# A field-pair interaction kernel: loading five blocks of x by GpSimd's queue, 120 rows in one transfer

## The chip, the cores and the metric

The kernel runs on one core of a Trainium2 chip. The metric is the device time of one execution in microseconds (us). Three executions of the kernel before took 1344.6, 1345.8 and 1345.83 us; the median is 1345.8. The profile is of one execution, with a span of 1343.8 us from the program's first instruction to its last.

The core has a matrix engine (TensorE, PE, with its weight loads PEld), a vector engine (VectorE, DVE), a scalar engine (ScalarE, ACT), GpSimd (POOL) and SyncE (SP). Sixteen DMA engines move data between the main memory and the core's own memory. They are fed by queues: SyncE and ScalarE each have one whose transfers are expanded by hardware, GpSimd has one that software expands. A transfer is split over up to sixteen DMA engines, each does its share as a row of packets, and the transfer has landed when the last of them has reported to its semaphore.

## The reference

```python
B, F, D = (4096, 32, 64)              # inputs; W has F*(F-1)/2 = 496 matrices of D x D
idx_i, idx_j = np.triu_indices(F, k=1)
vi = inputs[:, idx_i, :]
vj = inputs[:, idx_j, :]
vidots = jnp.einsum('bpd,pde->bpe', vi, W)
return vidots * vj
```

For each of 4096 rows and each of the 496 pairs (i, j) of fields with i < j, field i's vector of 64 numbers goes through the pair's own matrix, and the result is multiplied element by element with field j's vector. The output, 4096 x 496 x 64 floats, is 520 MB; x is 33.6 MB and W 8.1 MB.

## The kernel before

The rows are cut into 16 blocks of 256. A block lies in the core's memory as `xs`, 128 partitions with two rows of x each (`NB` = 2), so a partition holds 2 x 32 x 64 floats, 16 KB; what one partition gets of a block is called a row from here on, and a block has 128 of them. There are two such buffers. A half of a block (one of the two rows of x in each partition) is a pass `t`; 32 passes are made. Of W, `wT` holds the whole, turned once at the start.

In a pass the kernel goes through the pairs in 46 steps. For a step, TensorE multiplies turned fields (`xT`) with a run of the matrices into PSUM (line 244); then VectorE multiplies that with field j from `xs` and writes the output buffer `ot` (line 261). For some steps (`aside`) ScalarE copies PSUM out (line 258) and GpSimd multiplies (line 259). A pass has five groups of pairs, and each group fills one `ot` buffer of up to 105 pairs, which SyncE's queue stores (line 266): 3,360 KB for the two largest groups. There are three `ot` buffers, so a group can be computed only when the store from three groups earlier has landed.

The blocks of x are loaded one block ahead: `loads` says at which step. Blocks 0 and 1 come at the start by SyncE's queue. Of the rest, ScalarE's queue brings most in one transfer of 128 rows of 16 KB (`load_x`, line 76). Blocks 4, 7, 10 and 13 come otherwise (`load_fifteen`, lines 95 to 105): rows 0 to 119 (`SWR` = 120) by GpSimd's queue in two transfers, each with half the fields of every row (line 103), and the last eight rows as two small transfers of five and three rows by ScalarE's queue (line 99). 

`turn_engines` (lines 86 to 93) issues a tiny copy by GpSimd's queue, of 5, 17 or 11 rows with two single floats each, into a scratch tile that nobody reads. Its purpose lies in how that queue deals shares to the DMA engines: a copy's number of shares moves on the place at which the next copy's shares begin. It is called with 5 at the start, with 1 (17 rows) after each half of a block in `load_fifteen`, and with 11 at the end. `keep_in_program_order` makes GpSimd issue these copies in the order of the source.

A block of x that is loaded is needed two passes later, when its first fields are turned (line 143); a load is issued in the seventh step of a pass (block 2 in pass 3, block b from 3 on in pass 2b - 2).

Of the kernel before, what the change touches and what calls it, by code (L numbers as in the profile page):

```python
# [12 lines left out]
def kernel(  # L13
# [16 lines left out]
    nc = tc.nc  # L30

    B, F, D = x.shape
    P = 128
# [30 lines left out]
    xs = {}  # L64

    def rows_of(dram: bass.AP, blk: int) -> bass.AP:
        return dram[blk * NB * P : (blk + 1) * NB * P]

    def new_x(blk: int):

        xs[blk] = xpool.tile([P, 1 + NB * F, D], F32, tag="xs", name=f"xs_{blk}")
        nc.gpsimd.memset(xs[blk][:, 0, :], 0.0)  # L72

    def load_x(blk: int, eng, k0: int = 0, k1: int = NB):
        src = rows_of(x, blk).rearrange("(p k) f d -> p (k f) d", k=NB)
        eng.dma_start(out=xs[blk][:, 1 + k0 * F : 1 + k1 * F, :], in_=src[:, k0 * F : k1 * F, :])
# [4 lines left out]
    SWR = 120  # L81
# [4 lines left out]
    def turn_engines(k: int):  # L86
        n = k if k > 1 else 17
        c = used[0] % 8
        used[0] += 1
        src = x[: NB * n].rearrange("(p k) f d -> p k f d", k=NB)  # L90
        tc.keep_in_program_order(
            nc.gpsimd.dma_start(out=scratch[:n, :, c : c + 1], in_=src[:, :, 0, 0:1])  # L92
        )

    def load_fifteen(blk: int):
        rows = rows_of(x, blk).rearrange("(p k) f d -> p k f d", k=NB)
        dst = xs[blk][:, 1:, :].rearrange("p (k f) d -> p k f d", k=NB)
        for a, b in ((SWR, SWR + 5), (SWR + 5, P)):
            nc.scalar.dma_start(out=xs[blk][a:b, 1:, :], in_=rows[a:b].rearrange("p k f d -> p (k f) d"))
        for h in range(2):  # L100
            cut = slice(h * F // 2, (h + 1) * F // 2)
            tc.keep_in_program_order(
                nc.gpsimd.dma_start(out=dst[:SWR, :, cut, :], in_=rows[:SWR, :, cut, :])  # L103
            )
            turn_engines(1)


    wflat = w.rearrange("p d e -> p (d e)")
# [4 lines left out]
    def load_w(c: int, eng=nc.sync):  # L113

        a, b = wrows[c]
        pool, tag = ((opool, "ot"), (opool, "ot"), (const, "w3"), (const, "w3"))[c]
        raw[c] = pool.tile([P, D * D], F32, tag=tag, name=f"raw_{c}")
        eng.dma_start(out=raw[c][: b - a, :], in_=wflat[a:b])

    def order_w(c: int, k: int, copy):  # L120
        r = wrows[c][1] - wrows[c][0]
        rp = tpool.tile([P, EU, 2, D], F32, tag="tmp", name=f"rp_{c}_{k}")
        src = raw[c][:r, :].rearrange("p (d h e) -> p e h d", h=2, d=D)
        copy(rp[:r], src[:, k * EU : (k + 1) * EU])  # L124
        return rp

    def turn_w(c: int, k: int, rp, copy):
        r = wrows[c][1] - wrows[c][0]
        if c not in wT:
            wT[c] = const.tile([P, r, E2], F32, tag=f"w{c}", name=f"wT_{c}")  # L130
        pt = psum.tile([P, EU, P], F32, tag="ps", name=f"ptw_{c}_{k}")
        for n in range(EU):
            nc.tensor.transpose(  # L133
                pt[:, n, :r], rp[:r, n].rearrange("p h d -> p (h d)"), ident[:r, :r]
            )
        copy(wT[c][:, :, k * EU : (k + 1) * EU], pt[:, :, :r].rearrange("p e r -> p r e"))  # L136

    def turn_x(blk: int, k: int, q: int, copy):

        pt = psum.tile([P, RUN, P], F32, tag="ps", name=f"ptx_{blk}_{k}_{q}")  # L140
        for n in range(RUN):
            s = k * F + q * RUN + n
            nc.tensor.transpose(  # L143
                pt[:, n, :], xs[blk][:, s : s + 2, :].rearrange("p f d -> p (f d)"), ident
            )
        xT = xtpool.tile([P, RUN, P], F32, tag="xT", name=f"xT_{blk}_{k}_{q}")
        copy(xT, pt)  # L147
        return xT
# [41 lines left out]
    loads = {place[blk * NB, LATE]: blk + 1 for blk in range(2, NBLK - 1)}  # L190
# [12 lines left out]
    v, p, a = nc.vector.tensor_copy, nc.gpsimd.tensor_copy, nc.scalar.copy  # L203
# [9 lines left out]
    for s, (t, st) in enumerate(sched):  # L213
        blk, kt = divmod(t, NB)
        g, i, c0, m = steps[st]
        if s in loads:
            new_x(loads[s])
            if loads[s] % 3 == 1:
                load_fifteen(loads[s])
            else:  # L220
                load_x(loads[s], nc.scalar)
        for what, *args in due.get(s, ()):
            if what == "x":
                xT[tuple(args)] = turn_x(*args, a)
            elif what == "turn":
                turn_w(*args, rps.pop(tuple(args)), a)
            else:
                c, k = args
                rps[c, k] = order_w(c, k, (v, v, p, v)[c] if k % 2 == 0 else (v, v, p, a)[c])
                if (c, k) == (2, NU - 1):  # L230
                    load_w(3, nc.scalar)

        base, end = groups[g]
        pa = p0[i] + c0
        if pa == base:
            ots[t] = opool.tile([P, cap, D], F32, tag="ot", name=f"ot_{t}_{g}")
        ot = ots[t]
        ps = psum.tile([P, 2, CH, E2], F32, tag="ps", name=f"ps_{s}")
        for c, (lo, hi) in enumerate(wrows):
            lo, hi = max(pa, lo), min(pa + m, hi)  # L240
            if lo < hi:
                for h in range(2):
                    n = i + 1 - h
                    nc.tensor.matmul(  # L244
                        ps[:, h, lo - pa : hi - pa, :],
                        xT[blk, kt, n // RUN][h * D : (h + 1) * D, n % RUN, :],
                        wT[c][h * D : (h + 1) * D, lo - wrows[c][0] : hi - wrows[c][0], :],
                        start=True,
                        stop=True,
                    )  # L250
        o = pa - base
        j = 1 + kt * F + i + 1 + c0
        dst = ot[:, o : o + m, :].rearrange("p m (h e) -> p m h e", h=2)
        src = ps[:, :, :m, :].rearrange("p h m e -> p m h e")
        xj = xs[blk][:, j : j + m, :].rearrange("p m (h e) -> p m h e", h=2)
        if i in aside and c0 == 0 and s not in no_aside:
            tmp = tpool.tile([P, CH, 2, E2], F32, tag="tmp", name=f"tmp_{s}")
            nc.scalar.copy(tmp, src)  # L258
            nc.gpsimd.tensor_mul(dst, tmp, xj)  # L259
        else:  # L260
            nc.vector.tensor_mul(dst, src, xj)  # L261

        ends = (p0[2], end) if s < NS and (t, g) == (0, 0) else (end,)
        if pa + m in ends:
            n0 = p0[2] if len(ends) > 1 and pa + m == end else base
            nc.sync.dma_start(
                out=rows_of(out, blk).rearrange("(p k) n d -> p k n d", k=NB)[:, kt, n0 : pa + m, :],
                in_=ot[:, n0 - base : pa + m - base, :],
            )
# [28 lines left out]
```

## Time and profile before

| what | us or share |
|---|---|
| median time | 1345.8 us |
| span of the profile | 1343.8 us |
| mean rate of the DMA engines | 419 GB/s |
| bytes written to main memory / read | 520.09 MB / 41.68 MB |
| VectorE busy | 956.0 us (71%) |
| GpSimd busy | 544.7 us (41%) |
| GpSimd's transfers of half-rows (line 103) | 8, 960 KB each, median 31.5 us from issue to landing |
| ScalarE's whole loads (line 76) | 10, 2048 KB each, 17.3 us |
| stores of the largest groups (line 266) | 64, 3360 KB each, 16.3 us |

The page gives each engine's busy time; the span in 40 slices, a digit for each, with the DMA engines' busy share in tenths; the queues with packets, megabytes and the share of sixteen engines' time; the chain of work that ended last, followed back from the end; and a list of who waited for whom, with the total in us, the number of times and the longest wait. [...]

### The profile page before, as it was taken

How to read it: one execution, taken by the hardware profiler on the slowest of the kernel's cores; microseconds unless marked ns; L12 is line 12 of the kernel's file. 1: busy time of each engine (PE TensorE's matmuls, PEld its weight loads, DVE VectorE, ACT ScalarE, POOL GpSimd, SP SyncE). 2: the span in 40 equal slices, each digit the busy share in tenths (PEclk: the TensorE clock that was granted, in tenths of full speed). 3: DMA queues.
4: the chain of work that ended last, by engine and by line, in shares of the span. 5: the costliest groups of instructions: out<-in, count | busy, mean ns of one | idle time of the engine just before them, and what ended most of it. 6: DMA issues, size and time to landing. Idle time of an engine off the chain costs nothing.

```text
span 1343.8 us, 17902 instructions
## 1 busy us (share of the span) xinstructions
PE 1163.9 (87%) x7424; PEld 680.1 (51%) x7424; DVE 956.0 (71%) x1262; ACT 374.1 (28%) x367; POOL 544.7 (41%) x264
## 2 busy tenths in 40 slices
PE   6989889888898888888889888888988889989894
PEld 4555545545455454455445554444554545545552
DVE  5778767766677677776758777576876767767774
ACT  3432222223232232222232222232222323223321
POOL 1813424444243445333444434442444424344431
PEclk9989999999999899998989999899899989989997
DMA  9999999999999999999999999999999999999997
GB/s 394 371 427 410 427 422 433 429 421 430 422 430 426 431 427 407 427 424 429 432 420 424 404 424 431 425 430 416 419 421 411 428 425 427 423 423 431 423 415 320
DMA packets 28258, 562.95 MB, mean 419 GB/s; under 512 B 3456, under 2 KB 3456, under 8 KB 5504
## 3 DMA queue, kind: packets, MB, share of 16 engines
q1 hardware_dynamic: 24048, 530.59, 93.0%
q10 hardware_dynamic: 1632, 23.33, 4.2%
q0 software_dynamic: 2496, 7.88, 1.5%
q8 instruction: 58, 0.95, 0.3%
q14 instruction: 24, 0.20, 0.0%
HBM read 41.68 MB, written 520.09 MB: 418 GB/s over the span
## 4 chain that ended last, share of the span: by engine, by line
DMA 50%; PE 23%; DVE 16%; POOL 6%; issue 3%; ACT 1%; DVEq 0%; SPq 0%; POOLq 0%; ACTq 0%
DMA out_dram<-ot 50%; PE ps L244 18%; DVE ot L261 16%; POOL ot L259 5%; PE ptx L143 4%; PE ptw L133 1%; DMA raw<-in_L_rec_W_dram 1%; POOL scratch L92 1%; ACT tmp L258 1%; POOL xs L103 0%; DVE rp L124 0%; POOL rp L124 0%; DVEq L261 0%; ACT wT L136 0%; POOL xs L72 0%
## 5 line engine op out<-in xcount | busy, mean ns | idle before, releaser
L261 DVE TENSOR_TENSOR ot<-ps,xs 128x1024 f32<-128x1024 f32 (+15 forms) x1252 | 944.8, 810 | 356.8 <-DMA out_dram<-ot 193.8
L244 PE MATMUL ps<-wT,xT 64*128 64x512 f32 (+13 forms) x6272 | 1017.8, 467 | 122.4 <-DVE ot L261 110.7
L244 PEld LDWEIGHTS ps<-wT,xT 64*128 64x128 f32 x6272 | 552.7, 193 | 553.1 <-DVE ot L261 289.0
L259 POOL TENSOR_TENSOR ot<-tmp,xs 128x1024 f32<-128x1024 f32 x220 | 519.0, 2360 | 622.1 <-ACT tmp L258 438.7
L258 ACT COPY tmp<-ps 128x1024 f32<-128x1024 f32 x220 | 222.7, 1012 | 468.3 <-PE ps L244 401.2
L147 ACT COPY xT<-ptx 128x1024 f32<-128x1024 f32 x128 | 129.5, 1012 | 451.1 <-PE ptx L143 451.1
L143 PE MATMUL ptx<-ident,xs 128*128 128x128 f32 x1024 | 142.0, 283 | 35.9 <-DVE ot L261 27.5
L143 PEld LDWEIGHTS ptx<-ident,xs 128*128 128x128 f32 x1024 | 111.8, 143 | 82.5 <-issue 41.9
L72 POOL MEMSET xs<- 128x64 f32 x16 | 2.4, 151 | 148.5 <-DVE ot L261 148.5
L133 PE MATMUL ptw<-ident,rp 128*128 128x128 f32 (+1 forms) x128 | 18.6, 298 | 3.9 <-DVE rp L124 3.9
L133 PEld LDWEIGHTS ptw<-ident,rp 128*128 128x128 f32 (+1 forms) x128 | 15.6, 156 | 10.3 <-DVE rp L124 5.0
L136 ACT COPY wT<-ptw 128x1024 f32<-128x1024 f32 (+1 forms) x15 | 14.8, 984 | 20.9 <-PE ptw L133 20.9
L124 DVE COPY rp<-raw 128x1024 f32<-128x1024 f32 (+1 forms) x9 | 10.7, 1221 | 10.8 <-DMA raw<-in_L_rec_W_dram 10.8
L92 POOL DMA_DIRECT2D scratch<-in_r_inputs_dram x10 | 9.1, 908 | 0.2 <-issue 0.2
L124 POOL COPY rp<-raw 128x1024 f32<-128x1024 f32 x4 | 7.9, 1979 | 0.1
L124 ACT COPY rp<-raw 112x1024 f32<-112x1024 f32 (+1 forms) x3 | 5.9, 1958 | 5.0 <-POOL ot L259 3.2
L103 POOL DMA_DIRECT2D xs<-in_r_inputs_dram x8 | 6.0, 753 | 1.4 <-issue 1.4
L136 DVE COPY wT<-ptw 128x1024 f32<-128x1024 f32 x1 | 1.2, 1224 | 2.9 <-PE ptw L133 2.9
L147 ACT ACT_TABLE_LOAD x1 | 1.3, 1283 | 0.7 <-PEq L285 0.7
masks.py:197 POOL MEMSET ident<- 128x128 f32 x1 | 0.2, 204 | 0.3 <-POOLq L285 0.3
masks.py:199 POOL TENSOR_SCALAR_AFFINE_SELECT ident<-ident 128x128 f32<-128x128 f32 x1 | 0.3, 288 | 0.0
L285 POOL MEMSET const-float32-0.0<- 128x1 f32 x1 | 0.1, 93 | 0.3 <-issue 0.3
(3 smaller groups left out, 0.3 us busy)
## 6 DMA issues: line engine op xcount, KB each, us to landing
out_dram<-ot SPq DMA_DIRECT2D x64, 3360.0 KB, 16.3
out_dram<-ot SPq DMA_DIRECT2D x32, 3168.0 KB, 16.4
out_dram<-ot SPq DMA_DIRECT2D x32, 3104.0 KB, 17.0
out_dram<-ot SPq DMA_DIRECT2D x31, 2880.0 KB, 17.1
xs<-in_r_inputs_dram ACTq DMA_DIRECT2D x10, 2048.0 KB, 17.3
xs<-in_r_inputs_dram POOLq DMA_DIRECT2D x8, 960.0 KB, 31.5
raw<-in_L_rec_W_dram SPq DMA_DIRECT2D x3, 2048.0 KB, 17.1
xs<-in_r_inputs_dram SPq DMA_DIRECT2D x2, 1024.0 KB, 5.2
```

Of the source, the lines that this page charges most:

```text
L72: nc.gpsimd.memset(xs[blk][:, 0, :], 0.0)
L92: nc.gpsimd.dma_start(out=scratch[:n, :, c : c + 1], in_=src[:, :, 0, 0:1])
L103: nc.gpsimd.dma_start(out=dst[:SWR, :, cut, :], in_=rows[:SWR, :, cut, :])
L124: copy(rp[:r], src[:, k * EU : (k + 1) * EU])
L133: nc.tensor.transpose(pt[:, n, :r], rp[:r, n].rearrange("p h d -> p (h d)"), ident[:r, :r])
L136: copy(wT[c][:, :, k * EU : (k + 1) * EU], pt[:, :, :r].rearrange("p e r -> p r e"))
L143: nc.tensor.transpose(pt[:, n, :], xs[blk][:, s : s + 2, :].rearrange("p f d -> p (f d)"), ident)
L147: copy(xT, pt)
L244: nc.tensor.matmul(ps[:, h, lo - pa : hi - pa, :], xT[blk, kt, n // RUN][h * D : (h + 1) * D, n % RUN, :], wT[c][h * D : (h + 1) * D, lo - ...
L258: nc.scalar.copy(tmp, src)
L259: nc.gpsimd.tensor_mul(dst, tmp, xj)
L261: nc.vector.tensor_mul(dst, src, xj)
```

## The change

`load_fifteen` takes the blocks whose number is divisible by three (3, 6, 9, 12 and 15) in place of 4, 7, 10 and 13. In it, rows 0 to 119 go in one transfer with all fields. After one `turn_engines(1)`, the last eight rows follow on GpSimd's queue too, as two transfers with half the fields each, so ScalarE's queue has no part in these blocks. It is meant to spread the load of x over the sixteen DMA engines in a different way: with fewer transfers and with no whole rows on a few engines.

```diff
     def load_fifteen(blk: int):
         rows = rows_of(x, blk).rearrange("(p k) f d -> p k f d", k=NB)
         dst = xs[blk][:, 1:, :].rearrange("p (k f) d -> p k f d", k=NB)
-        for a, b in ((SWR, SWR + 5), (SWR + 5, P)):
-            nc.scalar.dma_start(out=xs[blk][a:b, 1:, :], in_=rows[a:b].rearrange("p k f d -> p (k f) d"))
+
+        def part(ps: slice, fs: slice):
+            tc.keep_in_program_order(nc.gpsimd.dma_start(out=dst[ps, :, fs, :], in_=rows[ps, :, fs, :]))
+
+        part(slice(0, SWR), slice(0, F))
+        turn_engines(1)
         for h in range(2):
-            cut = slice(h * F // 2, (h + 1) * F // 2)
-            tc.keep_in_program_order(
-                nc.gpsimd.dma_start(out=dst[:SWR, :, cut, :], in_=rows[:SWR, :, cut, :])
-            )
-            turn_engines(1)
+            part(slice(SWR, P), slice(h * F // 2, (h + 1) * F // 2))
...
-            if loads[s] % 3 == 1:
+            if loads[s] % 3 == 0:
                 load_fifteen(loads[s])
             else:
                 load_x(loads[s], nc.scalar)
```

## The prediction

> **What bounds the kernel now.** First the page's parts 1 to 3, which say which resource is full.
>
> ```profile
> PE 1163.9 (87%) x7424; PEld 680.1 (51%) x7424; DVE 956.0 (71%) x1262; ACT 374.1 (28%) x367; POOL 544.7 (41%) x264
> ...
> DMA  9999999999999999999999999999999999999997
> ...
> q1 hardware_dynamic: 24048, 530.59, 93.0%
> q10 hardware_dynamic: 1632, 23.33, 4.2%
> q0 software_dynamic: 2496, 7.88, 1.5%
> ```
>
> The DMA engines are over 90% busy in every slice but the last. q1 is SyncE's queue (the stores), q10 ScalarE's (loads of x), q0 GpSimd's, which the change edits. It moves 7.88 MB of 563, so its bytes cannot matter much; where they go can. Next the chain that ended last and the list of waits:
>
> ```profile
> DMA 50%; PE 23%; DVE 16%; POOL 6%; issue 3%; ACT 1%; DVEq 0%; SPq 0%; POOLq 0%; ACTq 0%
> ```
>
> ```profile
> DVE ot L261 <- DMA out_dram<-ot: 193.8, 96, 5.9
> POOL ot L259 <- DMA out_dram<-ot: 162.2, 69, 5.6
> ```
>
> Half of the chain is stores, and VectorE and GpSimd stand 96 and 69 times before a store that has not yet freed its `ot` buffer. A store counts as landed when the last of 16 engines is done, so I turned to the trace's semaphore records: when each of a store's 16 updates arrives. The view of issues gives one number per store (16.3 us to landing); the records below it give the spread of the sixteen, as us after the first:
>
> ```
> issued at   8th later   15th later   16th later
>   182.0        0.44        1.59         1.85
>   255.6        0.88        2.15         4.94
>   (block 4 loaded by the GpSimd queue, from 264.9)
>   297.2        1.36        2.90         3.42
>   329.6        1.69        2.79         4.40
>   502.2        0.22        1.76         7.64
>   (block 7, from 511.5)
>   533.3        0.46        2.71         3.76
>   748.1        0.13        1.74         7.64
>   (block 10, from 757.4; block 13, from 1003.8)
>  1326.5        0.07        1.43         6.42
> ```
>
> One engine lags alone. Its lag grows by about 0.27 us a store, and falls by 3 to 4 us whenever GpSimd loads a block. The packet records say why: a packet of 26,880 bytes takes 996 ns in most chains of packets, but 1,029 to 1,039 in one, and 8 x 34 ns = 0.27 us, the growth. That same chain is the one that gets 4-byte fillers on q0 in place of rows while `load_fifteen` runs:
>
> ```
> queue  start us   ns    bytes
>  q10   268.149    627   16384     one row of the five-row copy
>  q1    268.772   1021   26880
>  q0    269.796      9       4     filler: this engine gets none of the 120 rows
>  q1    269.802   1036   26880
>  q0    270.835      9       4
>  q1    270.840   1042   26880
> ```
>
> Is this engine ever idle? From 272.4 (its landing of the store issued at 255.6) to 1342.2 (its last) are 1,069.8 us. Its work there: 131 stores of 8 packets at the slow chain's times (1.03, 0.975, 0.955 and 0.887 us for the four sizes), 1,023 us; 8 loads of 8 rows at 0.627, 40; some 7 for the four odd rows, fillers and instruction fetches; together 1,070. It is never idle: **the time of this kernel is the work of one DMA engine**, and a row of x (16 KB) put on it costs 0.627 us, a row taken off it saves 0.627.
>
> **What the Trainium skill says.** "Perfetto Trace Analysis", section "What DMA-bound means", lists specific DMA engines among the things that can bind; the lag above agrees. "DMA: Bandwidth & Descriptors", section "Why a DMA increments its semaphore by 16 and not by 1", tells how engines are chosen. For a copy on k engines, k is the largest number up to 16 that divides the slowest dimensions; the hardware queues take the lowest-numbered k; GpSimd's takes k consecutive ones from a cursor that goes round. The trace agrees: a 17x2x1 copy shows one 136-byte packet (34 words), so k = 1; a 120x2x1024 copy shows 240 packets on 15 engines. The slow chain has a row of the five-row copy (engines 0 to 4) and none of the three-row copy (0 to 2), so it is engine 3 or 4. A cursor set to 5 by `turn_engines(5)`, if it starts at 0, makes 15 engines from 5 on leave out 4. The same section has an exception: GpSimd's queue gives "some direct copies" k = 16 with ceil(partitions/16) rows an engine, so that 100 partitions put data on engines 0-14. It does not say which copies. No run so far shows one: every GpSimd copy of the kernel before has two counting dimensions (x2x).
>
> **The change part by part.**
> (1) Four reliefs become five, in blocks 3, 6, 9, 12, 15.
> (2) The 120 rows go as one transfer. In the built program its form is 120x4096: the two halves of a row are adjacent on both sides and merge, so only one counting dimension is left. That is a plain row copy, the kind for which the exception's examples are given in bare partition counts. Under it ceil(120/16) = 8 rows go to each of engines 0 to 14, and number 15 gets none, wherever the cursor stands. Engine 4 then carries 8 rows where it carried none.
> (3) The last 8 rows go as two 8x2x1024 copies, k = 8 each, 16 engines in a row: half a row to every engine, the slow one included. They were 5+3 whole rows on engines 0 to 4 and 0 to 2.
> (4) `turn_engines(1)` once, not twice; two ACT issues (276 ns each) go. GpSimd issues four copies a block as before (some 0.75 to 0.97 us each, 3.5 us). Its multiply (L259) waits behind them, as before, and it is 41% busy: nothing. In later blocks a copy also waits for the semaphore of a transfer eight GpSimd copies back, as turns did before; that transfer landed some 200 us earlier: nothing.
>
> The ledger of rows on the slow engine, over 16 blocks of 8:
> - before: 12 blocks x 8, 4 blocks x 1 (from the five-row copy) = 100.
> - after, engine 15 left out: 11 x 8 + 5 x (8 + 0.5) = 130.5.
> - after, engine 4 left out: 11 x 8 + 5 x 0.5 = 90.5.
>
> Cost of the first: 28 rows x 0.627 = 17.6 us, and 2.5 rows as ten 4 KB packets at 163 ns = 1.6 us. Off go the 128 fillers, which cost about 12 ns each (1,042 against 1,029), 1.5 us. Net +17.7. All of it lies on the path, as the engine has no idle time to hide it. What is not shown is a 16 KB row by GpSimd's queue: as a single packet 0.611 (q10's usual) to 0.627, as four packets 4 x 163 = 0.652; over 40 rows from -0.6 to +1.0 us. I take 0.627. The load's landing goes from 41 us to about 15 to 20 (8 rounds of 1.6 us, as for ScalarE's loads, median 17.3); the block is needed only about 80 us later, so either is hidden. Forecast: 1345.8 + 17.7 = **1363.5 us**.
>
> **The rivals.**
> (A) The cursor rule holds for the single transfer: k = 15, the cursor moves 15 + 1 + 8 + 8 = 32, and engine 4 is left out five times. 9.5 rows x 0.627 = 6.0 us less: 1339.9, faster. For it: the rule holds for all copies the trace shows, and the turns add up to multiples of 16 only if k = 15. Against it: none of these copies is of the new form.
> (B) All 16 shares are dealt, but from the cursor. Then block 3 skips engine 4, and the cursor, moved by 33, skips 5, 6, 7 and 8 afterwards. 88 + 0.5 + 4 x 8.5 = 122.5 rows, +22.5: about +13 us, 1359. The "engines 0-14" of the page speaks against it.
> (C) No change: engines other than the slow one would have to set the end. The sum of 1,070 against 1,069.8 us speaks against it, and so does the last store, 5 us later on that engine than on any other. 1345.8.
>
> **How the numbers follow.** Forecast 0.83, A 0.11, B 0.04, C 0.02. Slower is forecast and B, 0.87; faster is A, 0.11; same is C, 0.02. For the range: the bounds of the row price give 1363 to 1365; the slow engine's pace varies (a packet of 1,021 to 1,042 ns), and the lag's ups and downs at the end are worth 3 us or so. B comes in at 1359. So 1355 to 1370; A stays out.
>
> **What would show it.** q0 must move 5 x 2.097 = 10.5 MB and q10 20.7 in any case. If I am right, the last landing's lag behind the other fifteen never falls at blocks 3, 6, 9, 12, 15; the chain of 4-byte fillers is one with 996 ns packets; the lag stands at 6 to 8 us from about 400 us on, and VectorE's wait for stores grows by some 15 us. If the lag drops by 4 us at 182, 428, 674, 920 and 1166 us, A is true and the step that failed is (2). Wrong altogether would be a lag that no longer sets the end, or a block of x that arrives too late (transposes waiting for the xs load).

## The result and the profile after

The changed kernel takes 1364.1 us (median of 4 executions, 1363.4 to 1365.1), the kernel before 1345.8 beside it. The ratio is 1.0138 with a 95% interval of 1.0122 to 1.0154: 18.3 us slower, where 17.7 were forecast. The profiled execution spans 1362.1 us.

The same lines of the page of the changed kernel as of the one before (busy time by engine, busy tenths of the DMA engines, then the queues with kind, packets, MB and share of sixteen engines' time):

```profile
PE 1176.8 (86%) x7424; PEld 689.1 (51%) x7424; DVE 956.9 (70%) x1262; ACT 374.0 (27%) x367; POOL 544.0 (40%) x268
...
DMA  9999999999999999999999999999999999999997
...
q1 hardware_dynamic: 24048, 530.59, 92.2%
q10 hardware_dynamic: 1424, 20.71, 3.7%
q0 software_dynamic: 1424, 10.50, 2.1%
```

No digit of the DMA line tells the two kernels apart: the line is a mean over sixteen engines, and one that is a little fuller doesn't show. The bytes have moved as intended: 2.6 MB from ScalarE's queue (q10) to GpSimd's (q0), and q1, the stores, carries what it carried before. Nothing more is moved in all. The chain that ended last still consists of stores for half of its length:

```profile
DMA 49%; PE 26%; DVE 17%; POOL 4%; issue 2%; ACT 0%; DVEq 0%; SPq 0%; POOLq 0%; ACTq 0%
```

VectorE's main group (busy us and mean ns of one, then its idle time and what ended most of it), the kernel before first, then the changed one:

```profile
L261 DVE TENSOR_TENSOR ot<-ps,xs 128x1024 f32<-128x1024 f32 (+15 forms) x1252 | 944.8, 810 | 356.8 <-DMA out_dram<-ot 193.8
```

```profile
L261 DVE TENSOR_TENSOR ot<-ps,xs 128x1024 f32<-128x1024 f32 (+15 forms) x1252 | 945.6, 809 | 374.1 <-DMA out_dram<-ot 192.8
```

The work is the same to 1 us; the idle time has grown by 17.3 us, about the whole loss. But the part put down to stores has not grown. The list of waits shows where it went; first two lines of the kernel before, then the changed kernel:

```profile
DVE ot L261 <- PE ps L244: 150.9, 226, 2.7
...
PE ps L244 <- DVE ot L261: 110.7, 46, 5.3
```

```profile
DVE ot L261 <- DMA out_dram<-ot: 192.8, 79, 6.9
DVE ot L261 <- PE ps L244: 171.3, 248, 1.4
POOL ot L259 <- DMA out_dram<-ot: 169.2, 64, 6.6
...
PE ps L244 <- DVE ot L261: 130.1, 43, 6.4
```

VectorE waited for stores 79 times, not 96, but longer at the worst (6.9 us against 5.9), and 20 us more for TensorE. TensorE in turn waited 19 us more for VectorE, which cannot empty PSUM while `ot` is not free. The last semaphore to come gets the whole wait in this list; who caused it is not told. The semaphore records tell it. Here are stores of the changed kernel, in us after the first of their 16 landings, as shown for the kernel before:

```
issued at   8th later   15th later   16th later
  414.1        0.12        2.08         7.18
  (block 6 by the GpSimd queue, from 432.0)
  461.4        0.10        2.24         6.24
  499.0        0.10        2.12         6.93
  664.4        0.10        2.11         7.19
  (block 9, from 682.2)
  711.0        0.18        2.11         6.61
 1165.2        0.08        2.05         7.23
  (block 15, from 1183.1)
 1212.4        0.12        2.30         6.29
 1344.7        0.22        2.02         6.38
```

One engine lags as before, but the loads of blocks 6, 9, 12 and 15 take little off its lag, which is 7.2 us before them and 6.2 to 6.6 after: in the kernel before it fell from 7.6 to 3.8 us across such a load. The packet records around block 6 show why. A record doesn't name its engine, so a chain is put together by taking for the next packet the one that starts where the last ended. Two chains:

```
            queue  start us   ns    bytes
slow chain   q1    434.215   1011   26880
             q1    435.222   1029   26880
             q0    436.248    611   16384    a row of x: this engine has its share
             q1    436.855   1028   26880
other chain  q1    434.410   1006   26880
             q1    435.412    996   26880
             q1    436.405   1506   26880
             q0    437.912      7       4    filler: this engine is left out
             q1    437.926   1527   26880
```

The left-out engine is one of the ordinary ones, and so it is in blocks 3, 9, 12 and 15: there too the chain of long packets carries rows. Also seen here: the rows go as single packets of 16 KB, and the left-out engine's own stores take 1,527 to 1,648 ns a packet between its fillers though it moves no row. I had not foreseen that.

### The profile page after: what moved, and what is told of

Read it like the earlier page. It is cut to its first block, busy times and chain, and to the rows that moved or that the text cites. A ratio compares the mean times of both kernels' runs of the same rounds, so it can differ in the third digit from the quotient of the medians.

```text
span 1362.1 us, 17892 instructions
## 1 busy us (share of the span) xinstructions
PE 1176.8 (86%) x7424; PEld 689.1 (51%) x7424; DVE 956.9 (70%) x1262; ACT 374.0 (27%) x367; POOL 544.0 (40%) x268
## 4 chain that ended last, share of the span: by engine, by line
DMA 49%; PE 26%; DVE 17%; POOL 4%; issue 2%; ACT 0%; DVEq 0%; SPq 0%; POOLq 0%; ACTq 0%
DMA out_dram<-ot 49%; PE ps L244 21%; DVE ot L261 17%; PE ptx L143 4%; POOL ot L259 3%; PE ptw L133 1%; DMA raw<-in_L_rec_W_dram 1%; DVE rp L124 0%; ACT tmp L258 0%; POOL rp L124 0%; DVEq L261 0%; ACT wT L136 0%; POOLq L259 0%; SPq L76 0%; SPq L266 0%
## 5 line engine op out<-in xcount | busy, mean ns | idle before, releaser
L244 PE MATMUL ps<-wT,xT 64*128 64x512 f32 (+13 forms) x6272 | 1032.1, 473 | 141.5 <-DVE ot L261 130.1
L244 PEld LDWEIGHTS ps<-wT,xT 64*128 64x128 f32 x6272 | 562.5, 197 | 576.8 <-DVE ot L261 309.9
```

The costliest lines, as they stand in the source:

```text
L244: nc.tensor.matmul(ps[:, h, lo - pa : hi - pa, :], xT[blk, kt, n // RUN][h * D : (h + 1) * D, n % RUN, :], wT[c][h * D : (h + 1) * D, lo - ...
```

## A ledger of the slow engine

To weigh each load, I took the time from a store's 16th landing to the next store's. Away from loads these steps are 8.20, 7.80, 7.62 and 6.99 us, to within 0.1, for the four store sizes in every kernel in which the slow engine is last. What the steps in the 50 us after a load have over this is what the load cost the slow engine. In the kernels in which it stays the last, the values repeat within some 0.6 us; the means below are from the loads after the first 400 us for the blocks in question, and after 500 us for 4, 7, 10, 13. The first such load of a kernel, when the slow engine lags little yet, reads otherwise: 6.0 us at block 3 in the changed kernel, 3.6 at block 4 in the kernel before.

| load | slow engine's rows | cost to it, us |
|---|---|---|
| 128 rows by ScalarE's queue (every kernel) | 8 | 4.9 |
| kernel before, block 7, 10, 13 | 1, fillers | 2.9 |
| changed kernel, block 6, 9, 12, 15 | 8 + 1/2 | 7.0 |

Five loads of 7.0 for 4.9 and four of 4.9 for 2.9: 10.5 + 8.0 = 18.5 us, against 18.3 measured (17.0 if the first loads are put in at their own values). The sum closes, but not with the prices that the prediction used. The experiments below test the ledger and look for the reasons of its odd entries.

## The experiments

The kernel before, run beside them, took 1346.7 us with the first four experiments, 1346.2 with the next four and 1346.5 with the rest. The edits are against the changed kernel, or against the kernel before where the heading names it.

**Form of the copy: two half-row copies again, all else as changed.**

```diff
-        part(slice(0, SWR), slice(0, F))
-        turn_engines(1)
+        for h in range(2):
+            part(slice(0, SWR), slice(h * F // 2, (h + 1) * F // 2))
+            turn_engines(1)
```

> The changed kernel with the 120 rows again as two half-row copies (two counting dimensions, a turn after each); blocks 3, 6, 9, 12, 15 and the last eight rows by GpSimd's queue stay. My theory: the form decides which engine is left out, so the slow engine is relieved again, 90.5 rows against 100 in the kernel before, 1345.8 - 6.0 = 1340 us, and the lag falls by 3 to 4 us at each such load. Rival (the blocks chosen, or the eight rows on GpSimd's queue, cost the time): 1360 to 1364 as in the changed kernel.

Measured: 1343.3 us, ratio to the kernel before 0.9976 (0.9966 to 0.9985). The lag falls again at these loads (6.6 to 3.1 us at block 6), and a load costs the slow engine 2.6 us. So neither the blocks chosen nor the eight rows on GpSimd's queue made the kernel slower; the merging of the two copies did, be it by their number or by their form. The gain is 3.4 us, not 6, as 2.3 us a load (4.9 - 2.6) and not 4.7 is saved.

**Number of copies: the 120 rows as two plain copies of 60.**

```diff
-        part(slice(0, SWR), slice(0, F))
+        part(slice(0, SWR // 2), slice(0, F))
+        part(slice(SWR // 2, SWR), slice(0, F))
```

> The changed kernel with its 120 rows as two plain copies of 60 whole rows. My theory: ceil(60/16) = 4 rows an engine, again on engines 0 to 14, so no relief of the slow engine: 1364 us, like the changed kernel. Rival (one large transfer is bad, two smaller ones are good): near 1340 to 1346.

Measured: 1360.5 us (1.0104, 1.0089 to 1.0119). No relief, with two transfers as with one. So two transfers are not enough for it; what the relieving copies have and these lack is the second counting dimension. It is some 3.6 us better than expected: a load costs 6.0 us, not 7.0.

**No GpSimd load at all.**

```diff
-            if loads[s] % 3 == 0:
+            if loads[s] < 0:
```

> No block by GpSimd's queue; all of blocks 2 to 15 as 128 whole rows by ScalarE's. My theory: 128 rows on the slow engine, 28 more than in the kernel before at 0.627 us, less 1.5 us of fillers: 1362 us; the changed kernel's new loads then give nothing and cost some 1.6 us. Rival (the new loads by GpSimd's queue themselves slow the kernel): clearly below 1364, near 1346.

Measured: 1355.3 us (1.0065, 1.0050 to 1.0080). Here the expectation failed, and with it my account of the sizes. Taking all relief away costs 8.6 us, half of what I had priced. The changed kernel loses 9.7 us more than this (18.3 against 8.6): its loads do not merely fail to help, they do harm. Its queues in the page show that all x now goes by ScalarE's (q10):

```profile
q10 hardware_dynamic: 2144, 31.20, 5.5%
...
q0 software_dynamic: 64, 0.00, 0.0%
```

**Which engine is left out: the kernel before, its cursor moved by one.**

```diff
-    turn_engines(5)
+    turn_engines(6)
...
-    turn_engines(11)
+    turn_engines(10)
```

> The kernel before with its first turn of 6 rows in place of 5 (and 10 in place of 11 at the end), nothing else. My theory: the cursor decides for copies with two counting dimensions, so the engine left out is the next one, and the slow engine carries 8 + 1 rows in the four blocks: 132 rows, 32 x 0.627 = 20 us more, less fillers: 1364 us. Rival (the load by GpSimd's queue helps as such, whichever engine it leaves out): 1346.

Measured: 1358.9 us (1.0090, 1.0075 to 1.0105). The same bytes by the same queue in the same blocks, with another engine left out: 12.3 us slower. So the relief of that one engine is all that the GpSimd loads of the kernel before are worth. The size is again below mine: the load costs 5.9 us (rows as 32 packets of 4 KB at 0.163 us, and one of 0.627, make 5.84), so 5.9 - 2.9 = 3.0 us is lost four times.

**One transfer with two counting dimensions.** A gap of four floats in the middle of `xs` keeps the two halves of a partition's row apart.

```diff
-        xs[blk] = xpool.tile([P, 1 + NB * F, D], F32, tag="xs", name=f"xs_{blk}")
+        xs[blk] = xpool.tile([P, (1 + NB * F) * D + GAP], F32, tag="xs", name=f"xs_{blk}")
...
-        part(slice(0, SWR), slice(0, F))
+        part(slice(0, SWR), slice(0, F * D))
```

> The changed kernel with four floats of gap between the two rows of x in a partition of xs, so that the 120 rows in one transfer keep two counting dimensions (120x2x2048, packets of 8 KB). One transfer, as in the changed kernel. My theory (the form decides): the slow engine is left out again, and the time is below the kernel before. If each filler costs the slow engine some 70 ns, as the first runs suggest, its 16 fillers a load in place of 32 make a load 1.5 us instead of 2.6, and the time 1338 us; if fillers cost nothing, 1343 as with two halves. Rival (one large transfer costs by itself): near 1364.

Measured: 1374.8 us (1.0213, 1.0198 to 1.0228), against both. The time says nothing on the form. In this layout the last small copy waits for the landing of the copy before it. Its wait, from the list of waits of this kernel:

```profile
POOL xs L110 <- DMA xs<-in_r_inputs_dram: 84.2, 5, 17.6
```

GpSimd stands still for 17 us five times, its multiplies queue behind (five of them then run in a row from 464.3 us), and at 464 us the stores have run dry. The lag, 6.5 us before block 6 and 0.2 after, proves nothing with the stores stopped in between. But which engine was left out can be read from the packets. The slow chain, known by its long packets, from 3 us after the issue at 437.7 us:

```
queue  start us   ns    bytes
 q1   440.849   1029   26880
 q1   441.875   1020   26880
 q0   442.891      9       4     filler
 q1   442.897   1066   26880
 q0   443.959      9       4     filler
 q1   443.965      9       4     the store's report to its semaphore
 q0   443.971      9       4     filler
 q1   443.977   1036   26880
 q0   445.010      9       4     filler
```

Here the slow engine gets fillers and no row, in this block as in 3, 9, 12 and 15. In the changed kernel, one transfer of the same 120 rows gives it rows. With the number of transfers the same, the form decides.

**Is a 16 KB packet of GpSimd's queue dear in itself? All 128 rows in one plain copy.**

```diff
-        part(slice(0, SWR), slice(0, F))
-        turn_engines(1)
-        for h in range(2):
-            part(slice(SWR, P), slice(h * F // 2, (h + 1) * F // 2))
+        part(slice(0, P), slice(0, F))
```

> Blocks 3, 6, 9, 12, 15 as one plain copy of all 128 rows by GpSimd's queue, no turn and no small copies. Theory S (a 16 KB packet of GpSimd's queue costs the slow engine about 0.2 us more than one of ScalarE's): five loads of some 6.6 us instead of 4.9, 1355.3 + 8.5 = 1364 us. Theory P (the small copies and the turn after the 120 rows make the cost): 1355, as with no GpSimd load.

Measured: 1354.2 us (1.0059, 1.0044 to 1.0074), the same as without GpSimd's queue; a load costs 4.85 us. The expectation's theory S is out: 16 KB packets of GpSimd's queue cost what ScalarE's do (mean 617 ns against 614 in the same run after 150 us). This run also answers a rival that the page of the changed kernel suggests: its TensorE is busy 13 us longer than before (1176.8 against 1163.9), at a granted clock of 0.947 against 0.959. Here TensorE is busy still longer, 1182.9 us at a clock of 0.943, and the kernel is 10 us faster than the changed one. The clock does not set the time.

```profile
q0 software_dynamic: 784, 10.49, 1.8%
```

**Are the small copies to blame? The last eight rows by ScalarE again.**

```diff
-        for h in range(2):
-            part(slice(SWR, P), slice(h * F // 2, (h + 1) * F // 2))
+        for a, b in ((SWR, SWR + 5), (SWR + 5, P)):
+            nc.scalar.dma_start(out=xs[blk][a:b, 1:, :], in_=rows[a:b].rearrange("p k f d -> p (k f) d"))
```

> The changed kernel with the last eight rows by ScalarE's queue, five and three, as before the change; 120 rows plain by GpSimd's queue and one turn. Theory S (the 16 KB packets cost): the slow engine carries 8 rows at some 0.83 us and one at 0.63: 1355.3 + 5 x 2.4 = 1367 us. Theory P (the small copies cost): 1355.3 + 5 x 0.63 = 1358.

Measured: 1364.2 us (1.0131, 1.0114 to 1.0148), as slow as the changed kernel. A load costs 6.9 us, 1.4 more than its nine rows should. The small copies are not to blame: moving the last eight rows to GpSimd's queue is worth nothing either way. With the run before it, the extra cost belongs to the 120-row copy, and to none of 128.

**Do the fillers eat the relief? The kernel before with four quarter-row copies.**

```diff
-        for h in range(2):
-            cut = slice(h * F // 2, (h + 1) * F // 2)
+        for h in range(4):
+            cut = slice(h * F // 4, (h + 1) * F // 4)
```

> The kernel before with its 120 rows in four quarter-row copies with a turn after each, so 64 fillers on the slow engine a load in place of 32, with the same bytes. If a filler costs 70 ns: a load of 2.9 us becomes 5.1, the relief is gone, and the time is about 1346 + 4 x 2.2 = 1355 us. If a filler costs 12 ns and the rest comes from the load's bytes on the other engines: 1347 to 1348.

Measured: 1346.35 us (1.0001, 0.9993 to 1.0010). Twice the fillers leave the time as it was, but this run doesn't price a filler: in 38 of the 50 stores issued from 766 to 1168 us the 16th landing is less than 0.25 us behind the 15th, and for the store issued at 1061.1 us the two last engines are ordinary ones (packets of 24,832 bytes in 921 ns; the slow chain's take 926 to 973). The kernel before tells more. At block 7, ten packets of 26,880 bytes between the slow engine's fillers took 999 to 1,051 ns during the first half-row copy, which is usual for it. During the second, seven of 24,832 bytes took 1,058 to 1,152 where 955 is usual, with fillers between them in the same way. So 12 ns for a filler may stand, and the lost relief is no matter of their number.

**Uneven dealing without a left-out engine: 112 and 16 rows.**

```diff
+        part(slice(0, 112), slice(0, F))
+        part(slice(112, P), slice(0, F))
```

(in place of the four copies of the changed kernel)

> Blocks 3, 6, 9, 12, 15 by GpSimd's queue as two plain copies of 112 and 16 rows: 7 + 1 = 8 rows on each of the 16 engines, none left out, no turn, no half rows. Theory D (rows that are not dealt the way a 128-row copy is dealt cost every engine more, some 0.2 us a 16 KB packet): such a load costs the slow engine 6.5 us instead of 4.9, 1354.5 + 5 x 1.6 = 1362 us. Theory L (what costs is the left-out engine, its fillers or the small copies): 1355, as with all 128 rows in one plain copy.

Measured: 1357.0 us (1.0080, 1.0065 to 1.0095), between the two. A load costs 5.2 us, 0.35 more than a 128-row copy with the same eight rows an engine. So other ways of dealing rows cost something, but far less here than with 120 rows.

**More relief: the half-row form in nine blocks, then in thirteen.** Both have the two half-row copies of the first experiment, and:

```diff
-            if loads[s] % 3 == 0:
+            if loads[s] in (3, 5, 6, 8, 9, 11, 12, 14, 15):
```

(with thirteen: `if loads[s] >= 3:`)

> The half-row form of the first experiment in nine blocks (3, 5, 6, 8, 9, 11, 12, 14, 15) instead of five. If each such load relieves the slow engine by the 2.3 us measured: 1355.3 - 9 x 2.3 = 1335 us, unless other engines become the last (their 16th-to-15th distance was only 0.2 us after such loads): then 1338 to 1343. If relief is not what helped: no gain over 1343.

> The same in all thirteen blocks from 3 on. By relief alone 1355.3 - 13 x 2.3 = 1325 us, but then the other fifteen engines carry half a row more a block and set the end: 1335 to 1345, no better than with nine.

Measured: 1339.8 us (0.9951, 0.9935 to 0.9968) with nine, 1346.1 (0.9999, 0.9991 to 1.0008) with thirteen. Nine is better than both kernels, by 6.7 us than the kernel before and by some 25 (6.7 + 18.3) than the changed one. The page of the kernel with nine blocks:

```profile
DMA  9999999999999999999999999999999999999998
...
q0 software_dynamic: 6400, 18.92, 3.6%
q10 hardware_dynamic: 848, 12.32, 2.3%
```

GpSimd's queue moves 18.9 MB here, 1.8 times what it moves in the changed kernel, and the time is some 25 us shorter: the bytes of the queue never were the cost. The records say what stops it. After 400 us the 16th landing is 0.9 us behind the 15th in the mean, with thirteen blocks 0.8, against 3.4 in the kernel before. The last landing of a largest store follows the one before, away from loads, in 7.94 and 7.92 us (median), not 8.20; 8 x 0.996 = 7.97 is the ordinary engines' pace. So the slow engine is no longer alone in being the last. Four more loads make it 6.3 us slower, though the half rows that they add to each engine come to 4 x 2 x 0.163 = 1.3 us; the rest is not explained. The waits of the kernel with nine blocks hardly differ from those of the slower kernels in total, which shows again how little that line tells here:

```profile
DVE ot L262 <- DMA out_dram<-ot: 193.9, 90, 7.4
```

**The blocks alone: the kernel before with blocks 3, 6, 9, 12, 15.**

```diff
-            if loads[s] % 3 == 1:
+            if loads[s] % 3 == 0:
```

> The kernel before with blocks 3, 6, 9, 12, 15 in place of 4, 7, 10, 13, nothing else: one part of the change alone. By the measured 2.0 us of relief a load, five instead of four: 1346 - 2 = 1344 us. By the recorded prices (4.4 us a load) it would be 1341.5. Rival (the blocks chosen are bad): slower than before.

Measured: 1344.2 us (0.9983, 0.9976 to 0.9990). This part of the change is a gain of 2.3 us.

The ledger against the times, as difference from the kernel before: five loads of the kind named, the others 4.9, and 4 x 2.0 us lost where blocks 4, 7, 10, 13 have no relief.

| kernel | cost a load, us | ledger, us | measured, us |
|---|---|---|---|
| changed | 7.0 | +18.5 | +18.3 |
| two plain copies of 60 | 6.0 | +13.5 | +13.8 |
| no GpSimd load | 4.9 | +8.0 | +8.6 |
| cursor moved (four loads) | 5.9 | +12.0 | +12.3 |
| 128 plain | 4.85 | +7.8 | +8.0 |
| last rows by ScalarE | 6.9 | +18.0 | +18.0 |
| 112 + 16 | 5.2 | +9.5 | +10.5 |
| two half-row copies | 2.6 | -3.5 | -3.4 |
| blocks alone | 2.8 | -2.5 | -2.3 |

Nine kernels within 1 us. As each cost was read from the same kernel's trace, this shows that the whole difference arises at the last landings after loads. That it is one engine's work rests on more: on the 16th landing, which after 400 us is 3.4 us behind the 15th in the mean in the kernel before and 5.0 in the changed one, on the chains, and on the moved cursor.

## Why the prediction was right, and which terms were off

- **The bound.** Right. A single engine whose store packets are 3% slower is never idle, and what is put on it shows in the time (the cursor moved by one: +12.3 us with nothing else changed). Two readings were loose: at block 4 the lag fell by 1.5 us only, from 4.9 to 3.4, and a 17x2x1 copy shows one packet of 136 bytes on each of the sixteen engines, 128 for eight copies. As 136 bytes are all 34 words of the copy, k = 1 still follows. What stands under "8th later" is the ninth landing, at most 0.1 us later.
- **The form decides who is left out.** Right. The merged 120x4096 copy leaves out an ordinary engine in every block; 120x2x1024, in two transfers, and 120x2x2048, in one, leave out the one at the cursor. The exception that the Trainium skill tells in "DMA: Bandwidth & Descriptors", section "Why a DMA increments its semaphore by 16 and not by 1", fits all runs with 120 or 60 whole rows. That it is engine number 15 which is left out, no run shows; only that it is not the slow one. Rival A (1340) is out by time and by the lag. Rival B (1359) is too near for its time to be trusted with prices that were off, but it wanted the slow engine left out in block 3, and there the slow chain carries 16 KB rows of 628 to 913 ns.
- **The relief lost.** Mis-sized: "28 rows x 0.627 = 17.6 us", less fillers, so some 4 us a load. Measured: 4.9 - 2.9 = 2.0 us a load, 8 us in all (8.6 by the run without GpSimd loads). A whole load's price was right (8 x 0.611 to 0.627 against 4.9). What was off is the cost of a relief load, taken as one row and fillers, 1.0 us; it is 2.9. The packets of the slow engine's own stores get longer while the other fifteen take in the second half-rows: at block 7, the two stores during that copy took 0.99 and 0.74 us more than usual, with nothing but fillers put on the engine. The row, the fillers and these two make 2.7 of the 2.9.
- **The new loads.** Mis-sized the other way: half a row more, "ten 4 KB packets at 163 ns = 1.6 us". Measured: 7.0 - 4.9 = 2.1 us a load, 10.5 in all. The range of -0.6 to +1.0 us that I gave for a GpSimd row of 16 KB was too narrow: the 600 rows of these loads, over fifteen engines, had a mean of 711 ns a packet. For 40 rows that is 3.4 us above 0.627 a row; the stores beside them took longer too.
- **The sum.** The two errors, -8 and +9, cancel. That the forecast of 17.7 met 18.3 is luck in the size, not in the direction: with the right prices the sum would have been 18.5.
- **The signs to look for.** The megabytes, the lag (6 to 8 us between loads, up to 10.5 across one) and the fillers came as forecast. "VectorE's wait for stores grows by some 15 us" did not; the idle time did (17.3), under another name. The loads landed a little later than the 15 to 20 us given (median, the last number of this line of the page), and still early enough for the block's use:

```profile
xs<-in_r_inputs_dram POOLq DMA_DIRECT2D x5, 1920.0 KB, 20.5
```

**What stays open.** Why a 120-row copy is dear. Mean times of a 16 KB row packet on q0 are 617 ns in a 128-row copy, 654 in 60 + 60, 666 in 112 + 16, 694 and 711 with 120. The Trainium skill, "SBUF — State Buffer", section "Door 1: The DMA port swizzle (why `[64,N]` ≈ `[32,N]`)", says that the partition number picks the port, and that in a 128-partition transfer each engine serves a port of its own. If so, rows dealt otherwise could have engines meet at ports, in loads and against stores. The runs agree that 128 rows are the cheap case, but none of them shows a port, and the order of the others is not derived. The same cause could hold for the stretched stores of a left-out engine; that is not shown either, nor why the second half-row copy stretches them and the first does not. Open, too, is what makes the slow engine slow (see the last section).

## What to carry to other kernels

When DMA engines are busy throughout, look at the spread of the sixteen landings of a transfer, not at its time alone: here one slow engine was the whole bound, and a few rows moved off it were worth more than the megabytes of a queue. Before merging small transfers into a large one, ask what their shape did: here two counting dimensions decided which engine was spared, and one larger, simpler copy took that away. And price a load by what the bound resource loses from one landing to the next across it, rather than by its own packets; both of my packet sums were off by 1.8 to 1.9 us a load.

## What the runs showed that was not expected

- The slow engine is slow only while the compute engines work. In the kernel before, its packets are long up to one of 1,052 ns that starts at 1325.7 us; VectorE's last multiply ends at 1326.5, and the fifteen packets of 26,880 bytes after that take 996 to 1,001 ns, as on any engine. In the changed kernel the same happens at 1344.7 us, and in eight further kernels at their last multiply. So something that goes on during the computing slows this engine; no run shows what.
- An engine that gets only fillers does not run free: its store packets took 1,527 to 1,648 ns, not 1,000, during the load of block 6 in the changed kernel.
- GpSimd's issuing instructions for the three copies of a load take 547 to 612 ns here, against 739 to 779 for the 120x2x1024 copies before; in the time this doesn't show.
- Relief in nine blocks gives 1339.8 us; with thirteen, where the slow engine is no longer alone in being the last, it is 1346.1.
